# Selective scans in rounds on one core: one shared product and one shared scan for two of the three channel groups, with the decays moved to SBUF

## The chip, the cores and the metric

The kernel runs on one core of a Trainium2 chip. A core has a matrix engine (TensorE, "PE" in the profile), a vector engine (VectorE, "DVE"), an activation engine (ScalarE, "ACT"), GpSimd ("POOL") and a queue engine (SyncE, "SP") that here only issues DMAs. They run side by side, each through its own list of instructions in order, and wait for each other by semaphores. SBUF is the working memory of 128 partitions; PSUM holds what TensorE writes. The metric is the device time of one launch in microseconds. Smaller is better.

## The reference, cut to what matters

The network has four layers on a batch of four images of 56 by 56 tokens with 96 channels. Layers 0 and 1 contain a selective state-space scan in four directions (rows, rows backward, columns, columns backward); layers 2 and 3 are attention and a quantized feed-forward part. The scans are what the change touches. For each direction, with 192 inner channels `d` and 16 states `n`:

```python
dt = softplus(dt_raw @ dtw + dtb)             # per token and channel
d_a = exp(dt * A)                             # decay, per token, channel and state
h = d_a * h + (dt * B) * u                    # along the 3136 tokens
y = sum over the 16 states of h * C           # then + u * D, over four directions
```

So 192 x 16 = 3072 recurrences of 3136 steps each, for four directions, four images and two layers.

## The kernel before, in words

**Chunks and rounds.** One direction of one image is cut into 7 chunks of 448 tokens (`CS`), which makes 2 x 4 x 4 x 7 = 224 chunks. A chunk has 8 rounds, numbered `r` = 0 to 7: two halves of the channels (`e`, 96 channels each) times four values of `q`. A round covers 96 channels and 4 states, laid out as 3 groups `g` of 128 partitions (4 states by 32 channels). There are 1792 rounds, and they run one after the other in `scans` (L595 to L714).

**One round on the engines.** TensorE spreads B over the partitions into one PSUM bank (`spread_b`, L580). VectorE multiplies `du` (dt times u) with it into `v`, group by group (L673). For the third group GpSimd makes this product a round ahead (L651), except in the rounds that `OWN` and `OWN_TAIL` list, in which VectorE makes all three. ScalarE turns dt into decays, one group at a time, into three PSUM banks `da` (`decay`, L643). VectorE then runs three scans in place, `v` <- `da`, `v` (L699). The last state of a chunk is kept by ScalarE (L703) and put into the first column of the next chunk's `v` (`carried`, L658). GpSimd multiplies the states with C for all three groups at once (`hc`, L709), and TensorE adds them over the states two rounds later (`add_up`, L737). Once in four rounds ScalarE copies the sums into `Y` (`keep_sums`, L744).

**Where the next chunk is made ready.** While a chunk runs, the following one is prepared in steps tied to `r` (`prepare`, L524; `prepare_on_scalar`, L552; `prepare_ahead`, L561): TensorE projects u into B, C and raw step sizes (L428), ScalarE copies them to `cf` (L467, L469), GpSimd takes the upper halves off two row blocks of `cf` (`split`, L593), so that B is held as a sum of bf16 parts, TensorE makes the step sizes (L480), ScalarE the softplus by Exp and Ln (L489, L490), GpSimd `du` (L496), and SyncE writes dt and `du` to DRAM (`park`) and reads them back spread over the partitions (`spread`, L513; `fetch` for B and C, L521).

**What sets the order.** The order of TensorE, ScalarE, VectorE and GpSimd instructions is as written: nothing reorders them. In each round there are two places, `yield "F"` and `yield "C"`, at which the other layers' work ("lanes": `load`, `middle`, `fuse`, `attend`) puts in instructions. A running backlog per engine (`spend`, `room`) lets an amount in only while ScalarE's backlog stays at or below 4.0 us (`ACT_LIMIT`), and 0.9 us of it are taken off per half round. ScalarE work of the lanes goes in at "F". The parts with Silu and Gelu load an activation table before them and the table of Exp and Ln after them (L768). Matmuls of zeros (L724) fill TensorE where `keep_busy` finds too little work. After the last scan (`late`) the rest of the lanes runs alone.

Of the kernel before, what the change touches and what calls it, by code (L numbers as in the profile page):

```python
# [11 lines left out]
F32 = mybir.dt.float32  # L12
# [8 lines left out]
HS = 56  # L21
L = HS * HS
# [11 lines left out]
TOKENS = slice(1, CS + 1)  # L34
# [4 lines left out]
OWN = (3, 4, 6)  # L39
OWN_TAIL = (3, 4)  # L40
# [124 lines left out]
class Net:  # L165
    def __init__(self, ctx, tc, aps, at, out):
# [8 lines left out]
        self.dg = None  # L175
# [5 lines left out]
        self.U = [self.big.tile([C, L], F32, name=f"U{e}") for e in range(NE)]  # L181
# [9 lines left out]
    def late(self):  # L191

        self.scan_pool.close()
        self.wp = self.pool("late", bufs=2)
        self.nw, self.nwin, self.depth, self.banks = LATE_NW, LATE_DEPTH, LATE_DEPTH, LATE_BANKS
        tags = (("ps", BANKS), ("da0", 1), ("da1", 1), ("da2", 1), ("pp", 1), ("b", 1), ("y", 1))
        self.ring = cycle([t for t in tags for _ in range(t[1])])

    def ps(self):
        tag, bufs = next(self.ring) if self.ring else ("ps", BANKS)  # L200
        return self.psum.tile([128, 512], F32, tag=tag, name=tag, bufs=bufs)
# [45 lines left out]
    def setup(self):  # L247
# [95 lines left out]
        with tc.tile_pool(name="stage", bufs=1) as st:  # L343
# [10 lines left out]
            self.some = self.upper(self.tiles["w128"][:, :CS])  # L354
            self.zeros = const.tile([128, C], BF16, name="zeros")
# [103 lines left out]
    def rows(self, ch):  # L459
# [5 lines left out]
        ch.cf = sp.tile([128, CS], F32, name="cf")  # L465
# [5 lines left out]
    def step_sizes(self, ch):  # L471

        nc = self.nc
        ch.cd = self.dram.tile([2 * NS, CS], F32, tag="cd", name="cd", bufs=3)
        nc.sync.dma_start(ch.cd, ch.cf[: 2 * NS])
        ch.pd = [self.step_size(ch, 0, self.pp())]

    def step_size(self, ch, e, ps):
        rows = slice(32, 32 + RANK[ch.l])
        self.nc.tensor.matmul(ps[:C], ch.par.wt[rows, C * e : C * e + C], ch.cf[rows], start=True, stop=True)  # L480
        return ps[:C]

    def softplus(self, ch, e):

        dt = self.sp.tile([C, CS], F32, name="dtc")
        self.nc.scalar.activation(dt, ch.pd[e], AF.Exp, bias=ch.par.dtb[:, e : e + 1])  # L489
        self.nc.scalar.activation(dt, dt, AF.Ln, bias=1.0)  # L490
        ch.dtc.append(dt)

    def times_u(self, ch, e):

        du = self.sp.tile([C, CS], F32, name="duc")
        self.nc.gpsimd.tensor_tensor(  # L496
            du.rearrange("p (a b) -> p a b", b=HS),
            ch.dtc[e].rearrange("p (a b) -> p a b", b=HS),
            self.in_order(self.U[e], ch.orient, ch.c * CS, CS),
            ALU.mult,  # L500
        )
        ch.duc.append(du)

    def park(self, l, t):
        d = self.dram.tile([C, CS], F32, tag="dd", name="dd", bufs=8)
        self.nc.sync.dma_start(d, t)
        l.append(d)

    def spread(self, l, d, name):

        t = self.sp.tile([128, NG, CS], F32, name=name)
        for s in range(4):
            self.nc.sync.dma_start(t[32 * s : 32 * s + 32], d.rearrange("(g d) t -> d g t", d=32))  # L513
        l.append(t)

    def fetch(self, ch, q):

        t = self.sp.tile([128, 2, CS], F32, name="cb", bufs=5)
        rows = ch.cd.rearrange("(k n) t -> n k t", k=2)
        for s in range(4):  # L520
            self.nc.sync.dma_start(t[32 * s : 32 * s + 32], rows[q + 4 * s].partition_broadcast(32))  # L521
        ch.cb.append(t)

    def prepare(self, ch, follow, r):  # L524

        if r == 0:
            self.spread(ch.du, ch.dud[1], "du")
            self.spread(ch.dt, ch.dtd[1], "dt")
            self.fetch(ch, 3)
        if follow is None:  # L530
            return
        if r == 1:
            self.step_sizes(follow)
            self.split(follow, 0)
        elif r == 2:
            self.split(follow, 1)
        elif r == 3:
            follow.pd.append(self.step_size(follow, 1, self.pp()))
            self.times_u(follow, 0)
            self.park(follow.dtd, follow.dtc[0])  # L540
        elif r == 4:
            self.times_u(follow, 1)
            self.park(follow.dtd, follow.dtc[1])
            self.park(follow.dud, follow.duc[0])
            self.spread(follow.dt, follow.dtd[0], "dt")
        elif r == 5:
            self.park(follow.dud, follow.duc[1])
            self.spread(follow.du, follow.dud[0], "du")
        if r > 4:
            self.fetch(follow, r - 5)  # L550

    def prepare_on_scalar(self, follow, r):  # L552

        if follow is None:
            return
        if r == 0:
            self.rows(follow)
        elif r in (2, 3):
            self.softplus(follow, r - 2)

    def prepare_ahead(self, far, r):  # L561

        if far is None:
            return
        if r == 2:
            self.parameters(far)
        elif r == 5:
            self.inputs(far)
        e = self.projected(far, r)
        if e in (0, 1):  # L570
            self.project_step(far, e)

    def projected(self, far, r):

        return r - (6 if far.first else 4)

    def spread_b(self, ch, q):

        ps = self.psum.tile([128, 512], F32, tag="b", name="b", bufs=1)[:, :CS]
# [754 lines left out]
```

## Time and profile before

| what | value |
|---|---|
| three runs, median | 8515.21 us (8499.94 to 8519.49) |
| profiled execution, first to last instruction | 8506.0 us; the page gives no other time of it |
| its place among the runs | between the lowest and the median run |
| first scan to last scan (L699, first and last start) | 120.6 to 8157.2 us |
| VectorE busy | 7810.2 us (92%) |
| GpSimd busy | 7589.0 us (89%) |
| TensorE busy, its mean clock | 7442.0 us (87%), 0.895 |
| ScalarE busy | 5928.4 us (70%) |

A group row of the page gives source line, engine, operation, what is written and read with shapes, and the count; behind the first bar the busy time of the group and the mean duration of one, behind the second the engine's idle time just before it and who ended that. The busy time of a group counts overlapping instructions once. In a timeline the first column is the start in us and the second the time until the last of the merged instructions ends.

### The profile page before, as it was taken

How to read it: one execution, taken by the hardware profiler on the slowest of the kernel's cores; microseconds unless marked ns; L12 is line 12 of the kernel's file. 1: busy time of each engine (PE TensorE's matmuls, PEld its weight loads, DVE VectorE, ACT ScalarE, POOL GpSimd, SP SyncE). 2: the span in 40 equal slices, each digit the busy share in tenths (PEclk: the TensorE clock that was granted, in tenths of full speed). 3: DMA queues.
4: the chain of work that ended last, by engine and by line, in shares of the span. 5: the costliest groups of instructions: out<-in, count | busy, mean ns of one | idle time of the engine just before them, and what ended most of it. 6: DMA issues, size and time to landing. Idle time of an engine off the chain costs nothing. (4 is left out here: it accounts for less than half of the span.)

```text
span 8506.0 us, 120303 instructions
## 1 busy us (share of the span) xinstructions
PE 7442.0 (87%) x33459; PEld 2707.3 (32%) x33459; DVE 7810.2 (92%) x10142; ACT 5928.4 (70%) x12597; POOL 7589.0 (89%) x4075
## 2 busy tenths in 40 slices
PE   6888888898889888898889988998899888998997
PEld 3222223232333223232233223333333333333345
DVE  5999999999999999999999999999999999999941
ACT  5877667676777657776677755667766777667746
POOL 4989999999999999999999999999999999999930
PEclk8888889898999889998899988999899898998986
DMA  5777677677777777776777777666776777767731
GB/s 142 167 186 186 164 186 182 153 173 168 189 172 179 163 182 175 178 171 161 184 180 176 166 174 171 165 164 165 185 177 160 165 173 185 178 156 166 175 83 45
DMA packets 951337, 1417.87 MB, mean 167 GB/s; under 512 B 176578, under 2 KB 943812, under 8 KB 949796
## 3 DMA queue, kind: packets, MB, share of 16 engines
q1 hardware_dynamic: 949888, 1408.37, 69.2%
q8 instruction: 263, 4.31, 0.2%
q14 instruction: 414, 3.39, 0.1%
q10 hardware_dynamic: 772, 1.80, 0.1%
HBM read 1141.42 MB, written 268.14 MB: 166 GB/s over the span
## 5 line engine op out<-in xcount | busy, mean ns | idle before, releaser
L699 DVE TENSOR_TENSOR_SCAN v<-da,v 128x449 f32<-128x449 f32 (+1 forms) x5376 | 5507.6, 1072 | 62.2 <-ACT v L658 36.2
L709 POOL TENSOR_TENSOR hc<-v,cb 128x1344 f32<-128x1344 f32 x1792 | 5166.6, 2884 | 366.5 <-DVE v L699 230.8
L643 ACT ACTIVATE da<-dt,na 128x448 f32<-128x448 f32 x5376 | 3392.7, 633 | 1409.7 <-DVE v L699 1372.7
L673 DVE TENSOR_TENSOR v<-du,b 128x448 f32<-128x448 f32 x4172 | 2331.4, 605 | 164.7 <-PE b L580 68.4
L737 PE MATMUL y<-hc,four 128*32 128x448 f32 x14336 | 1942.7, 617 | 3.7 <-POOL hc L709 3.6
L651 POOL TENSOR_TENSOR v<-du,cb 128x448 f32<-128x448 f32 x1204 | 1373.4, 1141 | 102.0 <-DMA cb<-cd 45.6
L724 PE MATMUL y<-w,zeros 128*96 128x448 bf16 x5117 | 1443.3, 399 | 0.0
L580 PE MATMUL b<-cf,sel 128*128 128x448 bf16 x1792 | 685.2, 382 | 861.9 <-DVE v L673 856.3
L724 PEld LDWEIGHTS <-zeros 128*96 128x96 bf16 x5117 | 631.2, 134 | 1300.0 <-issue 1142.7
L428 PE MATMUL pp<-U,wd 96*128 96x448 f32 x896 | 671.2, 836 | 13.7 <-DMA U<-u 13.7
L737 PEld LDWEIGHTS y<-hc,four 128*32 128x32 f32 x14336 | 297.0, 114 | 1206.0 <-issue 816.8
L733 PE MATMUL y<-Y,ident 96*96 96x448 f32 x672 | 540.2, 893 | 52.2 <-ACT Y L744 33.0
L496 POOL TENSOR_TENSOR duc<-dtc,U 96x448 f32<-96x448 f32 x448 | 559.2, 1248 | 5.1 <-ACT dtc L490 5.1
L881 PE MATMUL ps<-win,dg 64*64 64x220 f32 (+9 forms) x1962 | 507.9, 453 | 0.0
L480 PE MATMUL pp<-cf,wd 12*96 12x448 f32 (+1 forms) x896 | 484.3, 622 | 0.4 <-ACT cf L467 0.4
L703 ACT COPY carry<-v 128x3 f32<-128x3 f32 x1536 | 298.7, 194 | 262.4 <-DVE v L699 260.0
L489 ACT ACTIVATE dtc<-pp,wd 96x448 f32<-96x448 f32 x448 | 279.0, 623 | 273.9 <-PE pp L480 272.7
L593 POOL TENSOR_TENSOR cf<-cf 64x448 f32<-64x448 f32 x448 | 417.1, 931 | 35.3 <-ACT cf L467 0.3
L744 ACT COPY Y<-y 96x448 f32<-96x448 f32 x448 | 339.5, 758 | 39.2 <-PE y L737 37.4
L881 PEld LDWEIGHTS ps<-win,dg 64*64 64x64 f32 (+2 forms) x1962 | 229.7, 158 | 326.2 <-issue 267.4
L580 PEld LDWEIGHTS <-sel 128*128 128x128 bf16 x1792 | 186.7, 104 | 348.9 <-issue 284.5
L733 PEld LDWEIGHTS y<-Y,ident 96*96 96x96 f32 x672 | 116.5, 184 | 550.1 <-ACT da L643 244.2
(411 smaller groups left out, 5954.0 us busy)
## 6 DMA issues: line engine op xcount, KB each, us to landing
cb<-cd SPq DMA_DIRECT2D x3584, 112.0 KB, 4.3
dt<-dd SPq DMA_DIRECT2D x1792, 168.0 KB, 4.3
du<-dd SPq DMA_DIRECT2D x1792, 168.0 KB, 4.2
dd<-dtc SPq DMA_DIRECT2D x448, 168.0 KB, 2.0
dd<-duc SPq DMA_DIRECT2D x448, 168.0 KB, 2.1
U<-u SPq DMA_DIRECT2D x112, 168.0 KB, 4.7
z<-w SPq DMA_DIRECT2D x56, 224.0 KB, 3.2
u<-w SPq DMA_DIRECT2D x56, 224.0 KB, 3.5
```

The costliest lines, as they stand in the source:

```text
L428: self.nc.tensor.matmul(ch.ps.rearrange("p (a b) -> p a b", b=HS), ch.par.wx[:, e], self.in_order(self.U[e], ch.orient, ch.c * CS, CS), st ...
L496: self.nc.gpsimd.tensor_tensor(du.rearrange("p (a b) -> p a b", b=HS), ch.dtc[e].rearrange("p (a b) -> p a b", b=HS), self.in_order(self.U ...
L580: self.nc.tensor.matmul(ps, self.sel[:, q], self.upper(ch.cf), start=True, stop=True)
L643: nc.scalar.activation(da[g][:, TOKENS], ch.dt[e][:, g], AF.Exp, scale=ch.par.na[:, e, q, g : g + 1])
L651: nc.gpsimd.tensor_tensor(v[:, 2, TOKENS], ch.du[e][:, 2], ch.cb[q][:, 1], ALU.mult)
L673: nc.vector.tensor_tensor(v[:, g, TOKENS], ch.du[e][:, g], b, ALU.mult)
L699: nc.vector.tensor_tensor_scan(v[:, g, way], da[g][:, way], v[:, g, way], 0.0, ALU.mult, ALU.add)
L709: nc.gpsimd.tensor_tensor(hc, v[:, :, TOKENS], ch.cb[q][:, 0].unsqueeze(1).to_broadcast([128, NG, CS]), ALU.mult)
L724: self.nc.tensor.matmul(self.y[:C], self.zeros, self.some, start=False, stop=False)
L733: nc.tensor.matmul(o, w, self.in_order(a, ch.orient, ch.c * CS, CS), start=True, stop=False)
L737: nc.tensor.matmul(self.y[32 * n : 32 * n + 32], self.four, hc[:, g], start=n == 3, stop=n == 3 or q == NQ - 1,)
L881: self.nc.tensor.matmul(o[:, a - r0 : e - r0, x0:x1], diag[:, tap], win[:, a + dy - lo : e + dy - lo, x0 + dx : x1 + dx], start=n == 0, st ...
```

## The change

Groups 0 and 1 of a round now lie side by side in rows of 450 columns (`ROW`). Their product with B is one VectorE instruction into a PSUM tile `vp` over two banks, whose single copy serves all rounds, and their scan is one instruction over 899 columns, from decays that ScalarE now writes into SBUF (`da`, two copies, made two rounds ahead). Group 2 keeps its own scan, with decays in PSUM (`last`). The scan writes a new tile `h` and no longer works in place.

The state that a chunk takes over is no longer put into `v`: `carried` writes it into a column of `du` itself, and in the column beside the tokens B is 1, so that the product leaves the state as it is. `du` is one tile per `e` for the whole run. `carried(n + 2)` stands at the end of round `n`, after `decay(n + 1, 2)` and `kept(n)`, and the product of round `n + 1` is made in round `n`, between the two scans.

The upper half of B's parts is taken off by TensorE: `less` adds minus the bf16 part to the PSUM rows, and ScalarE copies the rest out; GpSimd's `split` is gone. The two `times_u` of a chunk become one, as do the two Ln and the two pairs of `park`. `OWN` loses one round. The diff, with removed lines mostly left out since they stand above:

```diff
--- before.py
+++ after.py
...
-TOKENS = slice(1, CS + 1)
+ROW = CS + 2
+WIDE = NG * ROW + 2
+INNER = slice(2, CS + 2)
+OUTER = slice(1, CS + 3)
+IN_VP = 60
...
-OWN = (3, 4, 6)
-OWN_TAIL = (3, 4)
+OWN = (3, 6)
+OWN_TAIL = (3,)
...
-        self.U = [self.big.tile([C, L], F32, name=f"U{e}") for e in range(NE)]
+        self.both = self.big.tile([C, NE, L], F32, name="U")
+        self.U = [self.both[:, e] for e in range(NE)]
...
+        tags = (("ps", BANKS), ("vp", 2), ("da", 1), ("pp", 1), ("b", 1), ("y", 1))
...
+            self.minus = const.tile([128, 64], BF16, name="minus")
+            nc.vector.tensor_scalar(self.minus[64:], self.ident[64:, 64:], -1.0, None, ALU.mult)
...
             na = p.na.rearrange("p e q g -> p (e q g)")
             nc.scalar.activation(na, p.alog, AF.Exp)
             nc.scalar.mul(na, na, -1.0)
...
+        ch.cf = sp.tile([128, CS], F32, name="cf", bufs=3)
         if ch.l == 0:
             nc.scalar.activation(ch.cf, ch.ps, AF.Copy, scale=self.cscale[:, ch.k : ch.k + 1])
         else:
             nc.scalar.copy(ch.cf, ch.ps)
...
+    def step_size(self, ch, e):
         rows = slice(32, 32 + RANK[ch.l])
...
+        ch.pd = self.pp()[:C]
+        self.nc.tensor.matmul(ch.pd, ch.par.wt[rows, C * e : C * e + C], ch.cf[rows], start=True, stop=True)
     def softplus(self, ch, e):
...
+        scalar = self.nc.scalar
+        if e == 0:
+            ch.dtc = self.sp.tile([C, NE, CS], F32, name="dtc", bufs=1)
+        scalar.activation(ch.dtc[:, e], ch.pd, AF.Exp, bias=ch.par.dtb[:, e : e + 1])
+        if e == NE - 1:
+            scalar.activation(ch.dtc, ch.dtc, AF.Ln, bias=1.0)
+    def times_u(self, ch):
+        ch.duc = self.sp.tile([C, NE, CS], F32, name="duc", bufs=1)
+        u = self.both.rearrange("p e (h w) -> p e w h" if ch.orient else "p e (h w) -> p e h w", w=HS)
+        lo = ch.c * CS // HS
+        in_rows = lambda t: t.rearrange("p e (a b) -> p e a b", b=HS)
+        self.nc.gpsimd.tensor_tensor(in_rows(ch.duc), in_rows(ch.dtc), u[:, :, lo : lo + CS // HS], ALU.mult)
+    def park(self, t):
+        d = self.dram.tile([NE, C, CS], F32, tag="dd", name="dd", bufs=6)
+        self.nc.sync.dma_start(d.rearrange("e p t -> p e t"), t)
+        return d
+    def spread(self, t, d):
         for s in range(4):
             self.nc.sync.dma_start(t[32 * s : 32 * s + 32], d.rearrange("(g d) t -> d g t", d=32))
...
+    def spread_dt(self, ch, e):
+        ch.dt.append(self.sp.tile([128, NG, CS], F32, name="dt"))
+        self.spread(ch.dt[e], ch.dtd[e])
+    def spread_du(self, ch, e):
+        self.spread(self.groups(self.du[e], 2)[:, :, :CS], ch.dud[e])
+    def groups(self, t, at):
+        return t[:, at : at + NG * ROW].rearrange("p (g t) -> p g t", t=ROW)
     def fetch(self, ch, q):
...
+        t = next(self.cb)
         rows = ch.cd.rearrange("(k n) t -> n k t", k=2)
         for s in range(4):
...
+            self.nc.sync.dma_start(t[32 * s : 32 * s + 32, :, INNER], rows[q + 4 * s].partition_broadcast(32))
         ch.cb.append(t)
...
+    def prepare(self, ch, o):
+        nc = self.nc
+        if o == -14:
+            self.parameters(ch)
+        elif o == -12:
+            self.inputs(ch)
+        elif o == -9:
+            ch.cd = self.dram.tile([2 * NS, CS], F32, tag="cd", name="cd", bufs=3)
+            nc.sync.dma_start(ch.cd, ch.cf[: 2 * NS])
+            self.less(ch, 64)
+        elif o == -8:
+            self.less(ch, 96)
+        elif o in (-7, -6):
+            self.step_size(ch, o + 7)
+        elif o == -5:
+            self.times_u(ch)
+            ch.dtd = self.park(ch.dtc)
+        elif o == -4:
+            ch.dud = self.park(ch.duc)
+            self.spread_dt(ch, 0)
+        elif o == -3:
+            self.spread_du(ch, 0)
+        elif o == 0:
+            self.spread_du(ch, 1)
+            self.spread_dt(ch, 1)
+        if -3 <= o <= 0:
+            self.fetch(ch, o + 3)
+    def prepare_on_scalar(self, ch, o):
+        if o == -10:
+            self.rows(ch)
+        elif o in (-9, -8):
+            part = slice(64 if o == -9 else 96, 128)
+            self.nc.scalar.copy(ch.cf[part], ch.ps[part])
+        elif o in (-7, -6):
+            self.softplus(ch, o + 7)
+    def projected(self, ch, o):
+        return () if o not in (-12, -11) else (o + 12,) if not ch.first else (0, 1) if o == -11 else ()
+    def less(self, ch, at):
+        self.nc.tensor.matmul(
+            ch.ps[at:], self.minus[at:, at - 64 :], self.upper(ch.cf[at:]), start=False, stop=True, skip_group_check=True
+        )
     def spread_b(self, ch, q):
...
+        self.nc.tensor.matmul(self.b[:, INNER], self.sel[:, q], self.upper(ch.cf), start=True, stop=True)
     def upper(self, x):
         return x.bitcast(BF16).rearrange("p (t h) -> p t h", h=2)[:, :, 1]
...
     def scans(self):
...
                         ch.n, ch.first = n, n == 0 and step == 0
                         ch.skip = n == 0
                         ch.last = n == 3 and step == NCS - 1
...
+                        ch.cb, ch.dt = [], []
                         chunks.append(ch)
...
         rounds = [(ch, e, q) for ch in chunks for e in range(NE) for q in range(NQ)]
...
+        per = NE * NQ
+        self.du = [sp.tile([128, WIDE], F32, name=f"du{e}", bufs=1) for e in range(NE)]
+        da = [sp.tile([128, NE * ROW + 2], F32, name=f"da{n}", bufs=1) for n in range(2)]
+        cb = [sp.tile([128, 2, CS + 4], F32, name=f"cb{n}", bufs=1) for n in range(5)]
+        none = sp.tile([128, NG], F32, name="none", bufs=1)
+        self.cb = cycle(cb)
+        vp = self.psum.tile([128, 1024], F32, tag="vp", name="vp", bufs=1)
+        vp = vp[:, IN_VP : IN_VP + NE * ROW + 2]
+        last = self.psum.tile([128, 512], F32, tag="da", name="da", bufs=1)[:, : CS + 4]
+        self.b = self.psum.tile([128, 512], F32, tag="b", name="b", bufs=1)[:, : CS + 4]
+        for t in (*self.du, *da, none, last):
             nc.vector.memset(t, 0.0)
+        for t in (self.b, *cb):
+            nc.vector.memset(t, 1.0)
+        def steps(n):
+            return [(ch, n - per * j) for j, ch in enumerate(chunks[max(0, n // per) : n // per + 3], max(0, n // per))]
+        def ahead(n, project):
+            for ch, o in steps(n):
+                for e in self.projected(ch, o):
+                    project(ch, e)
+        for n in range(-14, 0):
+            for ch, o in steps(n):
+                self.prepare(ch, o)
+            for ch, o in steps(n):
+                self.prepare_on_scalar(ch, o)
+            ahead(n, self.project_step)
         def decay(n, g):
+            if n < len(rounds):
+                ch, e, q = rounds[n]
+                out = da[n % 2][:, g * ROW :] if g < 2 else last
+                nc.scalar.activation(out[:, INNER], ch.dt[e][:, g], AF.Exp, scale=ch.par.na[:, e, q, g : g + 1])
+        def carried(n):
+            if n < len(rounds):
+                ch, e, q = rounds[n]
+                to = self.groups(self.du[e], 2)[:, :, CS : CS + 1] if ch.rev else self.groups(self.du[e], 0)[:, :, 1:2]
+                nc.scalar.copy(to, (ch.par.carry[:, e, q] if ch.step else none).unsqueeze(2))
+        def kept(n):
             ch, e, q = rounds[n]
...
+            if ch.step < NCS - 1:
+                end = 2 if ch.rev else CS + 1
+                nc.scalar.copy(ch.par.carry[:, e, q].unsqueeze(2), self.groups(hs[n], 0)[:, :, end : end + 1])
+        def own(n):
+            ch, e, q = rounds[n]
+            return NQ * e + q in (OWN_TAIL if ch.l and ch.i else OWN)
+        hs = {}
         def begin(n):
...
+            if n < len(rounds):
+                ch, e, q = rounds[n]
+                self.spread_b(ch, q)
+                hs[n] = sp.tile([128, WIDE], F32, name="h", bufs=3)
+                if not own(n):
+                    w = slice(2 * ROW + 1, 3 * ROW + 1)
+                    nc.gpsimd.tensor_tensor(hs[n][:, w], self.du[e][:, w], ch.cb[q][:, 1, OUTER], ALU.mult)
+        def products(n):
+            if n < len(rounds):
+                ch, e, q = rounds[n]
+                pairs = lambda t: t[:, 1 : 2 * ROW + 1].rearrange("p (g t) -> p g t", t=ROW)
+                b = self.b[:, OUTER]
+                nc.vector.tensor_tensor(
+                    pairs(vp), pairs(self.du[e]), b.unsqueeze(1).to_broadcast([128, 2, ROW]), ALU.mult
+                )
+                if own(n):
+                    w = slice(2 * ROW + 1, 3 * ROW + 1)
+                    nc.vector.tensor_tensor(hs[n][:, w], self.du[e][:, w], b, ALU.mult)
+        def scan(n, out, a, v, width):
+            way = slice(width + 1, 1, -1) if rounds[n][0].rev else slice(1, width + 1)
+            nc.vector.tensor_tensor_scan(out[:, way], a[:, way], v[:, way], 0.0, ALU.mult, ALU.add)
         self.exp_and_ln()
         self.tables = True
...
+        carried(0)
+        begin(0)
+        for n, g in ((0, 0), (0, 1), (0, 2), (1, 0), (1, 1)):
+            decay(n, g)
+        products(0)
+        carried(1)
         late = []
         for n, (ch, e, q) in enumerate(rounds):
             r = NQ * e + q
...
+            for c, o in steps(n):
+                self.prepare(c, o)
             self.half_round()
...
             strided = [1.5 + 1.5 * ch.orient] * (r % NQ == 2)
...
+            ahead(n, lambda c, _: strided.append(1.5 + 1.5 * c.orient))
+            self.spend((0.6, 0.7, 1.7, 0, 0, 0, 0.7, 0.6)[r], (0.4, 1.3, 1.3, 0, 0, 0, 0, 0.4)[r] + sum(strided))
             yield "F", n, r
...
+            for c, o in steps(n):
+                self.prepare_on_scalar(c, o)
             ended = late.pop(0) if len(late) == 2 else None
             if ended:
                 self.keep_busy(ended[2])
...
+            begin(n + 1)
             if ended:
                 self.add_up(*ended)
...
+            ahead(n, self.project_step)
             self.half_round()
...
+            h = hs[n]
+            scan(n, h, da[n % 2], vp, 2 * ROW - 1)
+            for g in range(2):
+                decay(n + 2, g)
+            yield "C", n, r
+            products(n + 1)
+            if ended and ended[2] == NQ - 1:
+                self.spend(0.6, 0)
+                self.keep_sums(*ended[:3])
+            scan(n, h[:, 2 * ROW :], last, h[:, 2 * ROW :], CS + 1)
+            decay(n + 1, 2)
+            kept(n)
+            carried(n + 2)
             hc = sp.tile([128, NG, CS], F32, name="hc", bufs=3)
...
+            nc.gpsimd.tensor_tensor(
+                hc, self.groups(h, 2)[:, :, :CS],
+                ch.cb[q][:, 0, INNER].unsqueeze(1).to_broadcast([128, NG, CS]), ALU.mult,
+            )
             late.append((ch, e, q, hc))
+            del hs[n]
         for ended in late:
             self.add_up(*ended)
         self.keep_sums(ch, e, q)
...
     shape, dtype = inputs["x"].shape, inputs["x"].dtype
     data, at = lay_out(inputs)
...
+    nc = _bacc.Bacc("TRN2", target_bir_lowering=False, num_devices=1, dynamic_dma_scratch_size=4096)
     arrays, aps = {}, {}
     for name, a in data.items():
         arrays[f"in_{name}_dram"] = a
```

## The prediction

> **What bounds the kernel now.** I read the page's busy times first, then its groups, the busy times by stage, the timeline of single engines in the middle of the run, and the waits of VectorE.
>
> ```profile
> PE 7442.0 (87%) x33459; PEld 2707.3 (32%) x33459; DVE 7810.2 (92%) x10142; ACT 5928.4 (70%) x12597; POOL 7589.0 (89%) x4075
> ...
> L699 DVE TENSOR_TENSOR_SCAN v<-da,v 128x449 f32<-128x449 f32 (+1 forms) x5376 | 5507.6, 1072 | 62.2 <-ACT v L658 36.2
> L709 POOL TENSOR_TENSOR hc<-v,cb 128x1344 f32<-128x1344 f32 x1792 | 5166.6, 2884 | 366.5 <-DVE v L699 230.8
> L643 ACT ACTIVATE da<-dt,na 128x448 f32<-128x448 f32 x5376 | 3392.7, 633 | 1409.7 <-DVE v L699 1372.7
> L673 DVE TENSOR_TENSOR v<-du,b 128x448 f32<-128x448 f32 x4172 | 2331.4, 605 | 164.7 <-PE b L580 68.4
> ...
> L651 POOL TENSOR_TENSOR v<-du,cb 128x448 f32<-128x448 f32 x1204 | 1373.4, 1141 | 102.0 <-DMA cb<-cd 45.6
> ```
>
> Between the first and the last scan (120.6 to 8157.2 us) 1792 rounds take 4.485 us each. There VectorE is the bound, with GpSimd close behind; busy times by stage:
>
> ```profile
> 3000.00:4000.00 1000.00, 865.90 (x3882) 293.56 (x3879) 970.03 (x1241) 710.36 (x1451) 938.43 (x493) 0.91 0.73 174
> 7000.00:8000.00 1000.00, 917.49 (x4275) 342.10 (x4267) 968.37 (x1263) 720.68 (x1627) 959.30 (x522) 0.91 0.72 173
> ```
>
> (PE, PEld, DVE, ACT, POOL.) VectorE's own timeline gives the true price of an instruction, from start to start:
>
> ```profile
> 4001.20 1.13 DVE L673 TENSOR_TENSOR v<-du,b 128x448 f32<-128x448 f32 x2
> 4002.24 3.05 DVE L699 TENSOR_TENSOR_SCAN v<-da,v 128x449 f32<-128x449 f32 x3
> 4005.21 1.66 DVE L673 TENSOR_TENSOR v<-du,b 128x448 f32<-128x448 f32 x3
> 4006.79 3.05 DVE L699 TENSOR_TENSOR_SCAN v<-da,v 128x449 f32<-128x449 f32 x3
> 4009.76 1.12 DVE L673 TENSOR_TENSOR v<-du,b 128x448 f32<-128x448 f32 x2
> ```
>
> Two products take 1.04 (0.52 each), three scans 2.97 (0.99 each). A round with two products is 4.01, with three 4.55. Neighbours overlap by 0.08: the instructions themselves last 0.605 and 1.07. Where one must wait for its predecessor, the setup shows another picture:
>
> ```profile
> 4.94 0.17 DVE L366 CAST b1q<-b1s 128x3 f32<-128x3 fp8e5 x1
> 5.02 0.14 DVE L368 CAST b2s<-c 96x1 fp8e5<-96x1 f32 x1
> 5.14 0.17 DVE L365 CAST b1s<-c 128x3 fp8e5<-128x3 f32 x1
> ```
>
> L368 is independent and starts 0.08 after L366, before its end. L365 overwrites what L366 reads, and starts 0.03 after L366's end. So a wait on the instruction just ahead costs about 0.08 + 0.03 = 0.115 us. ScalarE and its small copies:
>
> ```profile
> 4005.77 0.63 ACT L643 ACTIVATE da<-dt,na 128x448 f32<-128x448 f32 x1
> 4007.91 0.64 ACT L643 ACTIVATE da<-dt,na 128x448 f32<-128x448 f32 x1 [1.50 <-DVE v L699]
> 4008.48 0.18 ACT L658 COPY v<-carry 128x3 f32<-128x3 f32 x1
> ```
>
> ```profile
> DVE v L699 <- ACT v L658: 36.2, 64, 4.1
> ```
>
> The reader sees the state copied in (L658) early in round n, for round n+1; VectorE waited for it for only 36 us in the whole run (last fence, from the waits: total, times, longest).
>
> [...] 633 ns for decays into PSUM against 666 for an activation from SBUF to SBUF (L1126).
>
> **The change part by part.** T is the end of a round's last scan.
>
> *VectorE, merging.* The element rates are 0.467 of 0.52 for 448 product elements [...] and twice that, 0.935 of 0.99, for 449 scanned, so the fixed parts are about 0.055. A product over 900 is 0.938 + 0.055 = 0.99 for 1.04. A scan over 899 is 1.873 + 0.055 = 1.93 for 1.98. A round becomes 3.91 for 4.01: 0.10 x 1792 = 183 us less, if nothing waits. But `products(n + 1)` overwrites the one `vp` that the scan just ahead reads, as L365 does. With that wait the scan counts 1.873 + 0.132 (the fixed part of its 1.067) + 0.034 = 2.04, the round 4.02, and merging yields nothing (+18 us). The trace has no such pair on a tile that lives on, so it lies between -183 and +18; I take the wait. The product's write into PSUM across two banks is not shown either (L638's memsets write PSUM without penalty, 433 ns for 450 columns); I take no price[...].
>
> *VectorE, `OWN`.* One product per chunk moves to GpSimd: 224 x 0.53 = -119.
>
> *GpSimd.* -417 (L593), two `duc` of 1.25 become one of 2.2 (-60), 224 products of 1.10 (+246): 33.2 becomes 32.1 us per chunk against 34 to 35.9 of rounds. Not the bound on average, but lumpier, below.
>
> *TensorE.* Two `less` per chunk, 0.38 each (b's L580), +170; the amounts told to `spend` rise by 0.8, so 1.3 zero matmuls of 0.28 less, -80. Covered by its 856 us of waiting for VectorE before L580; without that cover, +90.
>
> *ScalarE.* Row copies +233, decays into SBUF 3584 x 0.03 = +108, more `carried` +46, one Ln for two -23: 70% becomes 74%. The total is covered by 1373 us of waiting at L643, the order is not. `carried(n + 2)` is now behind `decay(n + 1, 2)` and `kept(n)`, and VectorE needs it at 2.0 after T, before the middle of round n+1. Unloaded it ends at T + 0.03 + 0.58 + 0.10 + 0.18 = 0.89. From there, with A of lane and preparation work, ScalarE does A, two decays (1.24), and the same 0.89 after the next scan: 3.02 + A. VectorE wants it at 4.3 + 2.0 = 6.3. So A may be 3.28, and 2.4 in rounds with the copy to `Y` (0.9; r = 1 and 5). Before: decay 0.77, A, decay 0.58, copy 0.21, wanted at 4.49 + 1.04: A up to 3.97. The lanes' limit is 4.0, and they use it: a Silu or Gelu pair is 2 x 0.63 + 2 x 1.283 = 3.8, the single ones 3.2, Relu pairs 3.5. Counted between two rounds' decays, 204 stretches exceed 3 us (65 at r = 1, 63 at r = 5). Behind the blocked product stand the second scan, GpSimd's `hc` and ScalarE's next decays.
>
> *GpSimd's lump.* At r = 3 it runs hc 2.87, the double `duc` 2.2, the product 1.10, ending at T + 6.2, that is 1.7 to 2.2 after the next T. `carried(5)` overwrites a column this product reads, and ends 0.2 later; VectorE wants it at 2.0. Late by 0 to 0.45, I take 0.2: +45. ScalarE stands still meanwhile, so bursts at r = 4 and 5 start about 1 us late.
>
> A burst of 3.6 then stalls VectorE by 0.3 at r = 3, 1.4 at 4, 1.9 at 5 (Y copy), 0.3 to 0.9 elsewhere; r = 0 to 2 push long ones away by their own preparation (up to 1.7). Mean 1.1: 204 x 1.1 = 224, less the 40 (36.2 + 3.9) waited today: +184.
>
> *SyncE.* Same bytes, two parks for four. dt of e = 1 is needed one round earlier: in the timeline it is issued until 4.8 after the round's start and lands 4.3 later, 9.1, wanted at 2 x 4.49 + 2.0 = 11. Covered by 1.9; beyond it, ScalarE waits with `decay(3, 2)` behind. du of e = 0 is wanted half a round earlier, with similar cover. Taken at nothing.
>
> **Sum.** +18 - 119 + 184 + 45 = +128 on 8506: 8634. The median of the runs lies 9 above the profiled span: **8643, say 8640 us, 1.5% slower**.
>
> **The rivals.** (1) No wait between scan and product: -183 in place of +18, so 8433 + 9, about 8440. [...] Against: the setup pair. It decides once ScalarE's and GpSimd's bill stays under 302 us, 1.3 us per burst and lump. This is the one on the other side. (2) The chain through `carried` hardly bites, because bursts find VectorE late anyway (its rounds are 4.49, not 4.01): 0.3 per burst, lump nothing, -80: about 8435. For it: only 64 waits today. (3) Both: about 8240. (4) It bites harder, 2.2 per burst with PSUM writes dearer: about 8850. (5) The change is not what it says: were 900 columns as dear as two of 448, 0.105 more per round or 188, about 8830, counted with (4).
>
> **Chances.** Forecast 0.52 (8540 to 8760 its own range), (1) 0.18, (2) 0.14, (3) 0.04, (4) and (5) 0.12. Within 0.2%, about what a measurement of this kernel can tell from no change, 0.06 from the edges of (1) and (2); faster 0.28, slower 0.66. From 8415 to 8800 leaves out (3), half of (4) and the tails of (1) and (2).
>
> **What would show it.** Right: the long scan about 2.0 us, the product starting 0.03 after it; a new wait of VectorE's product on ScalarE's copy, over 150 us; GpSimd under 7400 busy. Wrong: products starting 0.08 before the scan's end, or no wait on the copy; VectorE 97% busy again in the middle stages at rounds of 4.3.

## Result and the profile after

| | before | after |
|---|---|---|
| median of the runs (four each) | 8510.20 us (8499.94 to 8519.49) | 8891.02 us (8870.85 to 8900.58) |
| profiled execution, span | 8506.0 us | 8869.1 us |
| start, to the first scan | 120.6 us | 116.1 us |
| first scan's start to last scan's end | 8037.7 us | 8368.9 us |
| last scan's end to the end | 347.7 us | 384.1 us |

The ratio is 1.0453, with a 95% interval of 1.0431 to 1.0476: 4.5% slower, where 1.5% was forecast, and above the top of the range (8800). On the profiled spans the 363 us are 331 between the scans, 36 in the tail behind them and -4 in the start.

The busy times and the main groups of the page after (columns as before: busy time and mean duration in ns of one, then the idle time just before them and who ended it):

```profile
PE 7829.7 (88%) x34344; PEld 2809.8 (32%) x34344; DVE 7633.0 (86%) x6344; ACT 6185.2 (70%) x13062; POOL 7412.8 (84%) x3627
...
L664 ACT ACTIVATE da<-dt,na 128x448 f32<-128x448 f32 x5376 | 3314.7, 652 | 1736.8 <-DVE h L710 1657.1
L710 DVE TENSOR_TENSOR_SCAN h<-da,vp 128x899 f32<-128x899 f32 x1792 | 3584.9, 2001 | 1.4 <-ACT da L664 1.4
...
L701 DVE TENSOR_TENSOR vp<-du,b 128x900 f32<-128x900 f32 x1792 | 1968.4, 1098 | 788.7 <-PE b L595 358.9
L710 DVE TENSOR_TENSOR_SCAN h<-da,h 128x449 f32<-128x449 f32 x1792 | 1942.7, 1084 | 0.0
```

No engine is full any more: VectorE went from 92% to 86% of a longer span, GpSimd from 89% to 84%. The instructions of VectorE cost less in sum (7810 to 7633 us), but the idle time before the product rose from 164.7 to 788.7 us. The scans themselves no longer wait for anything (1.4 and 0.0): whatever is late now stops the product. The busy times by stage (PE, PEld, DVE, ACT, POOL, with counts; then TensorE's granted clock, the DMA share and GB/s) show the same: VectorE is busy for 0.89 to 0.90 of these stretches, where it was 0.97.

```profile
3000.00:4000.00 1000.00, 873.86 (x3779) 291.04 (x3777) 903.40 (x727) 705.26 (x1436) 871.39 (x417) 0.88 0.68 166
7000.00:8000.00 1000.00, 914.86 (x4087) 333.53 (x4085) 885.81 (x736) 709.78 (x1582) 882.58 (x440) 0.89 0.67 162
```

VectorE's timeline after (start, duration, instruction; in brackets idle time that the profile puts down to someone):

```profile
4003.82 2.00 DVE L710 TENSOR_TENSOR_SCAN h<-da,vp 128x899 f32<-128x899 f32 x1
4005.95 1.10 DVE L701 TENSOR_TENSOR vp<-du,b 128x900 f32<-128x900 f32 x1
4006.96 1.08 DVE L710 TENSOR_TENSOR_SCAN h<-da,h 128x449 f32<-128x449 f32 x1
4007.97 2.00 DVE L710 TENSOR_TENSOR_SCAN h<-da,vp 128x899 f32<-128x899 f32 x1
...
4015.21 1.10 DVE L701 TENSOR_TENSOR vp<-du,b 128x900 f32<-128x900 f32 x1 [0.56 <-PE b L595]
```

From start to start the long scan takes 2.13 us, the product 1.01 and the short scan 1.01: a bare round is 4.15. The product starts 0.13 after the long scan has ended. The neighbours that follow the product overlap by 0.08 as before. Of the 1792 products 1416 directly follow the long scan. None of them starts before its end; 708 start 0.13 after it with nothing else waited for, and the others wait longer.

VectorE's waits after, then four of TensorE's after, then TensorE's largest before (total, times, longest):

```profile
DVE vp L701 <- PE b L595: 358.9, 317, 6.1
DVE vp L701 <- ACT du L671: 252.5, 237, 16.0
```

```profile
PE b L595 <- DVE vp L701: 185.1, 181, 12.2
PE y L786 <- POOL hc L754: 100.6, 120, 1.6
PE y L782 <- ACT Y L793: 94.9, 115, 3.9
PE pp L488 <- ACT dtc L498: 80.6, 74, 3.5
```

```profile
PE b L580 <- DVE v L673: 856.3, 681, 12.5
```

The wait for the spread B (`b`) was 68.4 us before. TensorE, which before waited 856 us for VectorE ahead of this matmul, now waits 185 there (222 with the product of the third group). Its idle time in all stayed as it was (span less busy time: 1064 us before, 1039 after), but it now stands at other places: the sum of its waits for ScalarE rose from 128 to 574 us, that of its waits for GpSimd from 20 to 116. A wait ahead of `b` in TensorE's list can make `b` late: with the state copied right behind the product (below), TensorE's wait for ScalarE's copy to `Y` rose from 95 to 373 us, and VectorE's wait for `b` from 359 to 563. Its mean clock also fell, from 0.895 to 0.879; whether that added to the lateness or came of the waiting was not separated.

The 331 us add up on VectorE. Between the first scan's start and the last scan's end its busy time fell by 189 us (7742 to 7553; the round that `OWN` lost is 119 of it by the forecast), and its idle time rose by 520 (296 to 816). The idle time ahead of products and scans accounts for more than all of the rise (211 to 774 us), and that ahead of the lanes' instructions fell (85 to 43). In the 774 the 708 bare gaps of 0.13 are 94 us; the rest is longer waits.

### The profile page after: what moved, and what is told of

Read it like the earlier page. It is cut to its first block, busy times and chain, and to the rows that moved or that the text cites. A ratio compares the mean times of both kernels' runs of the same rounds, so it can differ in the third digit from the quotient of the medians.

```text
span 8869.1 us, 115528 instructions
## 1 busy us (share of the span) xinstructions
PE 7829.7 (88%) x34344; PEld 2809.8 (32%) x34344; DVE 7633.0 (86%) x6344; ACT 6185.2 (70%) x13062; POOL 7412.8 (84%) x3627
## 5 line engine op out<-in xcount | busy, mean ns | idle before, releaser
L754 POOL TENSOR_TENSOR hc<-h,cb 128x1344 f32<-128x1344 f32 x1792 | 5181.9, 2892 | 926.1 <-DVE h L710 769.2
L664 ACT ACTIVATE da<-dt,na 128x448 f32<-128x448 f32 x5376 | 3314.7, 652 | 1736.8 <-DVE h L710 1657.1
L710 DVE TENSOR_TENSOR_SCAN h<-da,vp 128x899 f32<-128x899 f32 x1792 | 3584.9, 2001 | 1.4 <-ACT da L664 1.4
L701 DVE TENSOR_TENSOR vp<-du,b 128x900 f32<-128x900 f32 x1792 | 1968.4, 1098 | 788.7 <-PE b L595 358.9
L710 DVE TENSOR_TENSOR_SCAN h<-da,h 128x449 f32<-128x449 f32 x1792 | 1942.7, 1084 | 0.0
L693 POOL TENSOR_TENSOR h<-du,cb 128x450 f32<-128x450 f32 x1428 | 1641.1, 1149 | 89.6 <-DMA cb<-cd 59.6
L773 PE MATMUL y<-w,zeros 128*96 128x448 bf16 x5554 | 1547.2, 401 | 0.0
L671 ACT COPY du<-carry 128x3 f32<-128x3 f32 x1536 | 294.7, 192 | 331.0 <-POOL h L693 272.6
L508 POOL TENSOR_TENSOR duc<-dtc,U 96x896 f32<-96x896 f32 x224 | 518.6, 2315 | 1.8 <-ACT dtc L500 1.8
L838 PEld LDWEIGHTS ps<-avg,w 96*112 96x112 f32 (+2 forms) x1904 | 251.4, 198 | 187.3 <-issue 63.4
```

What stands on the lines that cost most here:

```text
L508: self.nc.gpsimd.tensor_tensor(in_rows(ch.duc), in_rows(ch.dtc), u[:, :, lo : lo + CS // HS], ALU.mult)
L664: nc.scalar.activation(out[:, INNER], ch.dt[e][:, g], AF.Exp, scale=ch.par.na[:, e, q, g : g + 1])
L693: nc.gpsimd.tensor_tensor(hs[n][:, w], self.du[e][:, w], ch.cb[q][:, 1, OUTER], ALU.mult)
L701: nc.vector.tensor_tensor(pairs(vp), pairs(self.du[e]), b.unsqueeze(1).to_broadcast([128, 2, ROW]), ALU.mult)
L710: nc.vector.tensor_tensor_scan(out[:, way], a[:, way], v[:, way], 0.0, ALU.mult, ALU.add)
L754: nc.gpsimd.tensor_tensor(hc, self.groups(h, 2)[:, :, :CS], ch.cb[q][:, 0, INNER].unsqueeze(1).to_broadcast([128, NG, CS]), ALU.mult,)
```

## Experiments

All kernels are edits of the changed kernel, and their ratios are to the kernel before, with 95% intervals. The theory to be tested was that the product's place between the two scans costs most: by the wait on the scan just ahead, and because B and the state column are then wanted one short scan, 1.0 us, earlier than behind the second scan. The rivals were a late state alone (chain), TensorE alone, the decays, GpSimd's load, and the zeros. The kernel before, timed again beside them, had medians from 8495 to 8507 us, so the times of different runs compare to about 15 us.

**Decays back in PSUM.** Product into `h`, scan in place, decays in one copy in PSUM, made a round ahead. So the product no longer overwrites what the scan just ahead reads.

```diff
-                out = da[n % 2][:, g * ROW :] if g < 2 else last
+                out = da[:, g * ROW :] if g < 2 else last
...
-                    pairs(vp), pairs(self.du[e]), b.unsqueeze(1).to_broadcast([128, 2, ROW]), ALU.mult
+                    pairs(hs[n]), pairs(self.du[e]), b.unsqueeze(1).to_broadcast([128, 2, ROW]), ALU.mult
...
-            scan(n, h, da[n % 2], vp, 2 * ROW - 1)
+            scan(n, h, da, h, 2 * ROW - 1)
             for g in range(2):
-                decay(n + 2, g)
+                decay(n + 1, g)
```

> The changed kernel with one thing undone: the decays of groups 0 and 1 go back to PSUM (one copy over two banks, one round ahead), the merged product writes the SBUF tile of the states, and the merged scan works in place there. The product no longer overwrites what the scan just ahead reads. Theory W (VectorE's wait on its own scan costs 0.215 us wherever nothing else is waited for): the product starts about 0.08 before the scan's end, and the run is 200 to 330 us faster than the changed kernel's 8890, so 8560 to 8690. Rival S (the waits for b and for the state column only move into the freed time): within 100 us of 8890.

Measured: 8885.98 us, 1.0462 (1.0440 to 1.0485), as slow as the change. That is in Rival S's range, but not by its waits: those for `b` and the column fell too (to 136 and 117 us). The timeline of VectorE in this kernel shows that the gap is gone (in its source the decays have the name `vp`):

```profile
4006.12 2.00 DVE L709 TENSOR_TENSOR_SCAN h<-vp,h 128x899 f32<-128x899 f32 x1
4008.04 1.07 DVE L700 TENSOR_TENSOR h<-du,b 128x900 f32<-128x900 f32 x1
4009.02 1.08 DVE L709 TENSOR_TENSOR_SCAN h<-da,h 128x449 f32<-128x449 f32 x1
4010.02 2.00 DVE L709 TENSOR_TENSOR_SCAN h<-vp,h 128x899 f32<-128x899 f32 x1
...
4016.19 2.03 DVE L709 TENSOR_TENSOR_SCAN h<-vp,h 128x899 f32<-128x899 f32 x1 [1.20 <-ACT vp L663]
```

The long scan counts 1.92 and the bare round 3.90, the unwaited figures of the prediction (1.93 and 3.91). But the last line shows what took its place: with one copy, ScalarE can't start on the next decays before the scan has ended, and the long scan waits 417.5 us for them. A wait went and a new one came, so this run proves the gap's cause but doesn't price it.

**B spread half a round earlier.** TensorE makes round n+1's `b` at the start of round n.

```diff
-                self.spread_b(ch, q)
...
+            if n + 1 < len(rounds):
+                self.spread_b(rounds[n + 1][0], rounds[n + 1][2])
             for c, o in steps(n):
```

> The changed kernel with the matmul that spreads B put at the start of TensorE's round, ahead of the lanes' matmuls and the zero matmuls, in place of behind them. Theory B (B comes late since it is now needed half a round sooner while TensorE still reaches it behind that work): VectorE's waits for b fall from 359 to under 100 us and the run is 150 to 280 us faster, 8610 to 8740. Rival A (ScalarE's state column is late in the same rounds): waits for b fall, those for the column grow, under 80 us gained.

Measured: 8807.39 us, 1.0365 (1.0345 to 1.0384), 84 us less than the change. The product's wait for `b` falls from 359 to 206 us, the one for the state column rises from 252 to 310. Both forecasts were missed, the second one narrowly. A late `b` is one part of the cause, well short of all of it.

**The state copied right behind the product.**

```diff
             products(n + 1)
+            carried(n + 2)
...
             kept(n)
-            carried(n + 2)
```

> The changed kernel with the copy of the taken-over state moved up on ScalarE, from behind the last decay and the kept state to just behind the next product, ahead of the copy to Y. Theory C (the place of the copy behind the round's last scan makes it late): VectorE's waits for du from ScalarE fall from 252 to under 100 us, 100 to 200 us faster, 8690 to 8790. Rival P (it is GpSimd's product of the third group that the copy waits for, 317 us of ScalarE's waits): ScalarE then stands still there ahead of the last decay, and the time is within 50 us of 8890 or above it.

Measured: 9050.60 us, 1.0656 (1.0636 to 1.0676), 160 us more. ScalarE's first waits in this kernel:

```profile
ACT du L671 <- POOL h L693: 1124.3, 768, 4.1
ACT da L664 <- DVE h L710: 715.8, 1118, 5.0
```

The copy overwrites a column that GpSimd's product still reads, so ScalarE stands still for it (1124 us, 317 in the change), with its decays and projection copies behind. VectorE's wait for the column falls to 141 us, but its wait for `b` rises to 563: TensorE now waits 373 us for ScalarE's copy to `Y` (95 in the change), so a late ScalarE reaches `b` through TensorE.

**No state at all.** `carried` is left out after the first two rounds, so chunks start without the state of the one before.

```diff
             kept(n)
-            carried(n + 2)
```

> The changed kernel with the copy of the taken-over state left out in all rounds but the first two, so that every chunk starts without the states of the one before: that part of the computation is missing. It gives the whole price of the chain from GpSimd's product over ScalarE's copy to VectorE's next product. Theory C: 180 to 260 us faster, 8630 to 8710. If the waits for b take its place: under 100 us faster.

Measured: 8686.83 us, 1.0224 (1.0204 to 1.0244), 204 us less than the change. The whole price of the state's path is 204 us in this order of work. The wait for `b` doesn't move:

```profile
DVE vp L701 <- PE b L595: 359.1, 343, 7.4
```

**The product behind the second scan.** One line moves; all the rest of the change stays.

```diff
-            products(n + 1)
             if ended and ended[2] == NQ - 1:
...
             scan(n, h[:, 2 * ROW :], last, h[:, 2 * ROW :], CS + 1)
+            products(n + 1)
             decay(n + 1, 2)
```

> The changed kernel with the product of the next round moved from between the two scans to behind the second. Then b and the state column are wanted 1.0 us later, the overwritten tile was read two instructions before, and it is the long scan that follows its own product directly. Theory D (the product's place between the scans is what is dear: too little slack for b and for the column, and a wait of 0.215 on the scan ahead against 0.115 for a single wait behind the product): waits of the product fall from 789 to under 300 us, 250 to 450 us faster, 8440 to 8640. Rival E (TensorE is full and late whatever the place): waits for b stay over 200 us and under 150 us are gained.

Measured: 8466.65 us, 0.9960 (0.9946 to 0.9974). That is 424 us less than the change, and 0.4% faster than the kernel before. VectorE's timeline, its group of products and its waits, and TensorE's wait for VectorE:

```profile
4010.67 2.03 DVE L710 TENSOR_TENSOR_SCAN h<-da,vp 128x899 f32<-128x899 f32 x1
4012.61 1.06 DVE L710 TENSOR_TENSOR_SCAN h<-da,h 128x449 f32<-128x449 f32 x1
4013.59 1.07 DVE L701 TENSOR_TENSOR vp<-du,b 128x900 f32<-128x900 f32 x1
4014.70 2.02 DVE L710 TENSOR_TENSOR_SCAN h<-da,vp 128x899 f32<-128x899 f32 x1
```

```profile
L701 DVE TENSOR_TENSOR vp<-du,b 128x900 f32<-128x900 f32 x1792 | 1933.9, 1079 | 214.1 <-PE b L595 132.4 <-ACT du L671 43.5 <-ACT w L1136 9.4
```

```profile
PE b L595 <- DVE vp L701: 400.9, 404, 12.4
```

The product now starts 0.08 before the short scan's end, since the scan whose input it overwrites is two instructions back. The long scan still waits for the product just ahead of it, whose result it reads. In 1063 of the 1428 such rounds it starts 0.03 after that product's end, as in the setup's casts, and in 362 it starts 0.10 after. The bare round is 4.03. The product's idle time falls from 789 to 214 us, and TensorE waits for VectorE again (401 us), so it is ahead once more; its waits for ScalarE sum to 205 us, against 574 in the change, and its mean clock is 0.903.

**B's parts split on GpSimd again.** `less` and the two row copies go, `split` comes back.

```diff
-            self.less(ch, 64)
+            self.split(ch, 0)
...
-            self.less(ch, 96)
+            self.split(ch, 1)
...
-            part = slice(64 if o == -9 else 96, 128)
-            self.nc.scalar.copy(ch.cf[part], ch.ps[part])
```

> The changed kernel with the split of B's parts back on GpSimd: no extra matmuls, no extra copies by ScalarE, two GpSimd operations of 0.93 per chunk more. Theory F (the split on TensorE made it wait for ScalarE, 189 us of waits at its matmuls of pp that were not there before, and these make b late): waits for b fall by 100 to 200, 50 to 150 us faster, 8740 to 8840. Rival G (GpSimd's time was needed; its lag lengthens the wait for the state column): 50 to 150 us slower.

Measured: 8920.13 us, 1.0496 (1.0476 to 1.0516), 29 us more. `b` is no earlier (364 us waited), so taking the extra matmuls off TensorE and the copies off ScalarE doesn't help when GpSimd has to do the work instead. It does not clear TensorE's waits for ScalarE: these stay (598 us, 574 in the change), 210 of them at the matmuls of `pp`, so the waits that Theory F blames were moved and not taken away.

**Both moves: product last, B early.**

> The product behind the second scan and B's matmul at the start of TensorE's round together. Theory D with B: a further 30 to 80 us below e5. Rival: with 1.0 us more slack b is in time anyway, within 20 us of e5.

Measured: 8528.58 us, 1.0036 (1.0021 to 1.0050), 62 us worse than the product's move alone. The wait for `b` falls from 132 to 71 us, and the scans' wait for decays rises from 72 to 121:

```profile
DVE h L709 <- ACT da L664: 120.7, 103, 11.8
```

So with the product last an earlier `b` wins nothing. These two waits nearly cancel (61 us less, 49 more), so they don't explain the 62 us, and their cause stays open.

**Product last, split on GpSimd.**

> The product behind the second scan and the split back on GpSimd together. If the split on TensorE is a cost of its own, 50 to 150 us below e5; if it mattered only through b, within 30 us of e5; if GpSimd then becomes the bound, above e5.

Measured: 8572.51 us, 1.0089 (1.0074 to 1.0104), 106 us worse than the product's move alone. Here GpSimd is the fullest engine (page's busy times):

```profile
PE 7571.8 (88%) x33896; PEld 2763.3 (32%) x33896; DVE 7657.4 (89%) x6344; ACT 5821.5 (68%) x12614; POOL 7810.7 (91%) x4075
```

So the move of the split to TensorE is worth having, once VectorE isn't held up.

**B early and no state, product still between the scans.** Both suppliers of the product are then out of the way, and what is left is its place.

> The changed kernel, its product still between the scans, with B's matmul early and the copy of the taken-over state left out after the first two rounds (chunks start without states, that part of the computation is missing). With most of both late inputs gone, what stays above e5's 8467 is the dearer wait on the scan just ahead. If lateness of b and of the column explains all of e5's gain: 8480 or below. If the wait of 0.215 against 0.115 counts as well (0.1 in some 1400 rounds): 8560 to 8640.

Measured: 8578.87 us, 1.0092 (1.0072 to 1.0111), 112 us more than with the product last and the states kept. That lies in the range named for the case that the wait on the scan ahead counts as well. Here 1207 of the 1416 products that directly follow the long scan start 0.09 to 0.11 after its end: the gap shrank a little with one wait fewer on the product.

**Product last, fewer zero matmuls.** `WARM` from 7.3 to 6.0.

> e5 with the target of the zero matmuls lowered from 7.3 to 6.0, so up to 1.3 fewer in three of four rounds. If TensorE's fullness (95% busy late in e5) still makes b late: waits for b fall under 60 us and 40 to 120 us gained, 8350 to 8430. If the zeros held TensorE's clock up: lower clock, 20 us or more slower.

Measured: 8466.14 us, 0.9960 (0.9946 to 0.9974). TensorE's busy time falls from 7615 to 7499 us and the time stays; the wait for `b` is 122 us instead of 132. But the median of TensorE's clock fell too, from 0.906 to 0.886, as the second theory had it. So fewer zeros gain nothing here; whether less work and a lower clock cancel was not separated, and with the product between the scans it was not tried.

**Product last, no state.**

> e5 with the copy of the taken-over state left out after the first two rounds (chunks start without states). In the changed kernel the copy cost 204 us. If the product's place took that away: within 60 us of e5's 8467. If the chain over GpSimd and ScalarE still costs its own time: 100 us or more faster.

Measured: 8406.80 us, 0.9900 (0.9878 to 0.9922), 60 us less than with the states. The same path that costs 204 us with the product between the scans costs 60 with the product last.

**`times_u` in two halves**, the second one a round later, against GpSimd's lump.

```diff
-            self.times_u(ch)
+            self.times_u(ch, 0)
             ch.dtd = self.park(ch.dtc)
         elif o == -4:
+            self.times_u(ch, 1)
```

> The changed kernel with GpSimd's one product of dt and u over both halves cut into two again, the second a round later. The prediction put 45 us on the lump that the single one makes at r = 3. If that holds: 20 to 100 us faster, 8790 to 8870, and ScalarE's waits for GpSimd (317 us) fall. If the lump is hidden, or the later second half makes du late: within 20 us of 8890, or slower.

Measured: 8952.22 us, 1.0519 (1.0486 to 1.0551), 61 us more. The edit lengthened two waits, since the transfers behind the second half go out later: ScalarE waits 156 us for `dt` (53 in the change) and 139 for `du` (62).

```profile
ACT da L666 <- DMA dt<-dd: 155.8, 101, 12.0
...
ACT du L673 <- DMA du<-dd: 139.0, 107, 9.8
```

ScalarE's wait for GpSimd's product falls from 317 to 273 us, but the wait for the state column stays (246 us). The lump was neither shown nor excluded by this.

**What the runs say together.** Four of them make a table (us):

| | state carried | no state |
|---|---|---|
| product between the scans | 8891 | 8687 |
| product behind the second scan | 8467 | 8407 |

The place costs 424 us with states and 280 without; the states cost 204 or 60. The 144 us in which they differ belong to both: the product stops for the column because it comes 1.0 us earlier. Of the 280, an early B takes back 108 (8687 to 8579). The other 172 (8579 to 8407) are what the place costs with `b` made early and no state awaited. The wait on the scan just ahead is part of that: a bare round is 4.11 us there and 4.04 with the product last, which over 1416 rounds would be some 100 us. The product's wait for `b` is also 119 us longer there (first line; the second is the run with the product last and no state):

```profile
DVE vp L700 <- PE b L595: 236.0, 199, 5.8
```

```profile
DVE vp L701 <- PE b L595: 116.7, 131, 6.4
```

Together these are more than the 172, so the pure price of the wait stays open.

## Why the prediction was wrong

The direction was right, the size was not. Two steps failed, both about the product's new place: TensorE's 856 us of waiting were counted as cover for what it feeds VectorE, and the wait on the scan just ahead was priced at half of what it costs. The forecast without its two state terms (184 + 45) would be 8411 us; the run without states took 8687. So the miss of 251 us is not in the state's path. It lies in what the forecast charged to the product's place (a wait of 0.115 us, and nothing for `b`), and a little in the tail. How the 251 divide between the gap and `b` was not separated.

**"VectorE, merging"**: the durations held (long scan 2.00, product 1.01 start to start; into two banks of PSUM the product counts 1.01, into SBUF 0.98 in the run with the decays in PSUM, so that write cost at most 0.03). Taking the wait was right, and rival (1), without it, fell: no product that directly follows the long scan starts before its end. The wait is one for VectorE's own semaphore in the list of instructions; whether the overwrite needs it, no run shows. Its price was the mis-sized term. The prediction took 0.08 + 0.03 from a pair of casts; the product starts 0.133 after the end, so the price is 0.213 and the bare round 4.15, not 4.02. The casts stand behind one semaphore, and so do the 1063 long scans that start 0.03 after their product in the run with the product last. The product waits for three (its own engine, TensorE, ScalarE), and the trace shows a separate semaphore instruction of 50 ns ahead of it for two of them, 39 ns after the scan's end. The gain of merging itself is real: 3.90 in the run with the decays in PSUM.

**"TensorE"**: this step failed in kind. It named 856 us of waiting as cover for the new matmuls. Yet `products(n + 1)` now stands one scan (1.0 us) earlier on VectorE, while TensorE reaches `b` at the same place of its own list, behind results of scans and of ScalarE that come no earlier. The wait for `b` was the largest single one (359 us, 68 before). The cover shrank to 185, while TensorE's waits for ScalarE rose from 128 to 574 us. Taking the new matmuls away didn't help, bringing `b` forward did (84 and 108 us), and so did moving the product back, which also brought the waits for ScalarE down to 205. No run took these waits alone away, so their share in the lateness of `b` is argued from the traces and not measured. The prediction priced the lateness of the state by its deadline, and `b` by an idle total. The zeros rose by 437 instead of falling by some 290 (1.3 x 224); why stays open, and with the product last fewer of them gained nothing.

**"ScalarE" and "GpSimd's lump"**: forecast at +184 and +45, 229 together; leaving the states out gave 204. The mechanism is shown too: the product waits 252 us for ScalarE's copy (sign: over 150), and ScalarE 317 us for GpSimd's product ahead of it. How much is the lump stays open. Rival (2), in which the chain hardly bites, is out.

**"GpSimd"**: busy 7412.8 us, against the sign of under 7400; `duc` took 2315 ns for the 2.2 us assumed. Not the bound, as said. **"`OWN`"**: 224 products of VectorE less, as said. **"SyncE"**, taken at nothing: ScalarE waits 62 us for `du` (12 times) and 53 for `dt` (9 times), so its cover did not always hold, and the run with two halves shows what going past it costs.

**Not in the forecast**: the tail. After the last scan 384 us remain instead of 348. From 8490 us to the end TensorE works 318 us; before, in the stretch from 8165 us to its end, 292. More of the lanes' work was left for the end. That amounts told to `spend` have risen, and so let less of it in between, is only a guess.

**The rivals**: (4), at 8850, came nearest in time and by half in mechanism: harder, but by the wait and by `b`, not by dearer writes to PSUM (at most 0.03 us a product). Its own terms (204 x 2.2 - 40 in place of 184) make 8868, not 8850, before any dearer write. (5) is out: 900 columns cost less (1.01 us) than two of 448 (1.04).

## What to carry to other kernels

Idle time of an engine covers new work only if the place where its result is wanted stays where it was; when a consumer is moved forward, ask for every input when its maker reaches it, not how much time the maker has in sum. Don't put an instruction that overwrites a buffer right behind the one that reads it: with something independent between them the wait cost nothing here (the product started 0.08 before the short scan's end), and without it 0.2 us per round. The move of one line turned 4.5% slower into 0.4% faster, so a large change should be tried in more than one order before its parts are judged.

## What the runs showed of the hardware

- How late an instruction starts that waits for the one just ahead differed with the semaphores it waits for: 0.13 us after the end here (708 products, three semaphores, the wait for VectorE in a semaphore instruction of its own), 0.09 to 0.11 with one fewer (1207 products), and 0.03 with a single one (1063 long scans with the product last, and the setup's casts); 362 further long scans, whose wait for VectorE stands in a separate semaphore instruction, started 0.10 after. Independent neighbours overlap by 0.08. Against that overlap a wait cost up to 0.21 us here.
- A product over 900 columns into two banks of PSUM takes 1.01 us start to start, and a scan over 899 takes 1.92 unwaited. The prediction's sums of the elements and one fixed part were 0.99 and 1.93. The rates of the elements in it were the author's estimate, 0.467 us for 448 product columns and 0.935 for 449 scanned. Measured start to start, a product into SBUF goes from 0.52 us for 448 columns (before) to 0.98 for 900 (the run with the decays in PSUM) and a scan from 0.99 for 449 to 1.92 for 899, and these slopes give 0.46 and 0.93.
- The 3584 decays written into SBUF take 660 ns on average and the 1792 written into PSUM by the same kernel 636 (the group's 652 is the mean of both), a difference of 4%.
